# Two attention layers on one core: layer 1's value product by halves twice, its row sums on two engines, and three edits of order in every such product

## The chip, the cores and the metric

The kernel runs on one core of a Trainium2 chip. The metric is the device time of one launch in microseconds (us), as the median of three runs; less is better. A profile is one further execution.

## What is computed

Eight images of 512 channels and 1024 pixels (32 x 32) go through two attention layers, all in fp32. Layer 0 has 32 normalization groups and 8 heads, layer 1 has 8 groups and one head.

```python
# layer 0, per image
h = group_norm(x, 32 groups); q, k, v = w_qkv @ h + b
a = softmax((q * s).T @ (k * s)) @ v        # per head of 64 channels
x = x + w_proj @ a + b_proj
# layer 1
xn = group_norm(x, 8 groups)
q, k, v = (conv1x1(xn, w) for w in (q_w, k_w, v_w))
attn = softmax(einsum('bqc,bck->bqk', q, k) / sqrt(C))
x = x + conv1x1(einsum('bqk,bkc->bqc', attn, v), p_w, p_b)
```

In layer 1 the kernel multiplies the weights first: m is the product of the query and key weights, z's weight that of the value and projection weights. So it needs g = m h, the scores g h, z = h z_w, and the product of the exponentials with z, divided by the row sums.

## The kernel before

**Products in halves.** A matrix product is split in halves in each of its dimensions and made from seven products of halves instead of eight, by sums of the operands' quarters made ahead (`left_sums`, `right_sums`, lines 150 to 175) and additions to the results. Done once, this is `wino` (L222): seven steps, 1, 6, 2, 5, 7, 4, 3, on three kinds of PSUM banks a, b and c, with additions (L240, L251, L385, L387) as evictions. Done twice, it is `conv2` with `inner_steps`: four pairs of outer products, (1, 5), (2, 6), (7) and (3, 4), which its text numbers 0 to 3; each pair makes its inner steps on two outer products at a time that lie side by side in one PSUM bank.

**A pair in `inner_steps`.** Step 1 fills bank a. ScalarE copies a to b (L471), so that b goes on from the same product. Then come the previous pair's steps 3 and 4, held back in a list called `tail`, then this pair's 6, 2, 5 and 7. Step 6 adds to b and is evicted as u2, step 2 to a, step 5 fills c and is evicted as c5, step 7 adds to b and is evicted with c5. Step 3 adds to c and is evicted with u2, step 4 to b. Evictions of pair 0 are ScalarE copies (L461), the others VectorE additions (L539, with the bias L537), one for each outer product where the targets do not lie side by side, so two of 256 columns each. For pair 2 GpSimd adds results further (L544). A step 7's matmul writes bank b, so it waits until u2 has been read.

**Who uses which.** `conv2` makes layer 0's v (by tokens: image columns are the stationary operand and 128 weight columns stream), k, q and the projection p, and layer 1's g. v, k, q and p are made so 7 times, g 8 times. z is made by `by_token`, so by `wino`: 56 matmuls of 256 columns. `scores1` makes the 49 outer-inner products of the scores through `inner_steps`, with exponentials (L741) put into the hooks. `values1` is one `wino` (L828, L829 and L806 are its evictions).

**The order around z.** For image b in layer 1 and image b + 1 in layer 0 the order on TensorE is attention of layer 0, g, scores, z, the value product, then v, k, q and p. Instructions of an engine run in the order of the program where `keep_in_program_order` holds them. Small work that may lie anywhere goes to the list `background`: each step takes the first entry off it (three after a step of z). `hooks` are run after step 7 of each pair, or after a step of `wino`. z's first products lie between the last steps of the scores, and its last ones inside the value product.

**Row sums and factors.** The sums over the exponentials' rows for each of two column halves come from two quarters each (`add_up`, L745, all on GpSimd: two additions of 1024 columns, a third of 1024, one of 512). A small matmul with ones adds up over partitions. `right_sums` makes the right operand's factors from the exponentials in eight subtractions of 1024 columns (L788), four on VectorE, then four on GpSimd, which come after the sums in the `background`. The sums of z for the left operand (L157 to L160) run on VectorE.

**Weights.** Weight sums are made once at the start and kept in DRAM: `wdram` once halved (for z 1792 KB in one load), `wdram2` twice halved (1792 and 1344 KB in two loads, L337). `uses` lists the loads in their order; each `load_weight` takes the next. z's sums are made in image 0's attention, by entries of `later` indexed by the half head steps.

Of the kernel before, what the change touches and what calls it, by code (L numbers as in the profile page):

```python
# [9 lines left out]
F32 = mybir.dt.float32  # L10
# [19 lines left out]
def two_attention_blocks_kernel(  # L30
# [143 lines left out]
    def main_path(ctx):  # L174
# [124 lines left out]

        wdram2 = {n: dram.tile([P, 7, 7, P], F32, name=f"sums2_{n}") for n in "qkmvp"}  # L300

        def keep2(n, t, engine=nc.gpsimd):

            if engine is nc.gpsimd:
                u = wpool.tile([P, 4, 7, P], F32, tag="w", name=f"prepare2_{n}")
                u = [u[:, i, :, :] for i in range(4)]
            else:
                u = [big_tile(f"prepare2_{n}_{i}", (P, 7, P)) for i in range(4)]
            quarter = lambda k, i: t[:, :, k, ts(i, P)]
            a11, a21, a12, a22 = quarter(0, 0), quarter(0, 1), quarter(1, 0), quarter(1, 1)  # L310
            s1, s2, s3, s4 = u
            for dst, x, y, op in (
                (s1, a21, a22, ALU.add), (s2, s1, a11, ALU.subtract), (s3, a11, a21, ALU.subtract),
                (s4, a12, s2, ALU.subtract),
            ):
                tc.keep_in_program_order(engine.tensor_tensor(dst, x, y, op))
            for j, f in enumerate((a11, a12, s4, a22, s1, s2, s3)):
                nc.sync.dma_start(wdram2[n][:, :, j, :], f)

# [3 lines left out]
        for b in range(1, B - 1):  # L323
            uses += [*twice["m"], "z", *layer0, *twice["p"]]
        uses += ["p", *twice["m"], "z"]
        uses += [*twice["m"], "z"]
        loaded = []
# [15 lines left out]
        def weight_part(n):  # L343
            name, t = loaded.pop(0)
            assert name == n
            return t
# [93 lines left out]

        def inner_steps(uid, parity, k, mm, add, y, x, extra, after7, final, early=()):

# [22 lines left out]
            def step(j):  # L465
                if j == 1:
                    bank("a")
                    mm(ps["a"], 1, True)

                    bank("b")  # L470
                    nc.scalar.copy(ps["b"], ps["a"])  # L471
                elif j == 6:
                    mm(ps["b"], 6, False)
                    put([keep_tmp("u2", "u")], "b", (0, 1))
                    extra(0, 1, True, False)
                elif j == 2:
                    mm(ps["a"], 2, False)
                    put(y(0, 0), "a", (0, 0))
                    extra(0, 0, True, True)
                elif j == 5:  # L480
                    bank("c")
                    mm(ps["c"], 5, True)
                    put([keep_tmp("c5", "w")], "c", (1, 1))
                    extra(1, 1, True, False)
                elif j == 7:
                    mm(ps["b"], 7, False)
                    add(y(1, 1), ps["b"], [tmp["c5"]])
                    extra(1, 1, False, True)
                elif j == 3:
                    mm(ps["c"], 3, False)  # L490
                    add(y(0, 1), ps["c"], [tmp["u2"]])
                    extra(0, 1, False, True)
                elif j == 4:
                    mm(ps["b"], 4, False)
                    put(y(1, 0), "b", (1, 0))
                    extra(1, 0, True, True)
                run_background(1)
# [3 lines left out]
            for g in early:  # L501
                g()
            for j in (6, 2, 5, 7):
                step(j)
# [4 lines left out]

        def conv2(n, f, bias, name, hooks=(), after=(), by_tokens=False):  # L510

# [15 lines left out]

            def add(dst, ps, x):

                n = max(len(dst), len(x))  # L530
                for i in range(n):
                    d = dst[i] if len(dst) == n else dst[0][:, i : i + 1, :]
                    psi = ps[:, i : i + 1, :] if n > 1 else ps
                    xi = x[i] if len(x) == n else x[0][:, i : i + 1, :]
                    if isinstance(d, tuple):
                        d, oc = d
                        nc.vector.scalar_tensor_tensor(d, psi, bias[:, oc : oc + 1], xi, ALU.add, ALU.add)  # L537
                    else:
                        nc.vector.tensor_add(d, psi, xi)  # L539

# [12 lines left out]
            def pair(s, products, y, x, final):  # L553
# [20 lines left out]
                def extra(r, cc, read, done):  # L574
# [7 lines left out]
                    f"{name}_{s}", s % 2, len(products), mm, add, written, x and (lambda *at: blocks(x, *at)),  # L582
                    extra, hooks.pop(0) if hooks else (), final,
                )

            weights2 = [weight_part((n, 0))]
            pair(0, (1, 5), [(1, 0), (1, 1)], None, [])
# [124 lines left out]
        def scores1(f, gf, gsteps, first, uid, stats):  # L712
# [7 lines left out]
            total = pair_tile(f"sum_{uid}")  # L720
            parts = [pair_tile(f"sum{r}_{uid}") for r in range(2)]
            g2 = {1: first}
# [20 lines left out]
            def add_up(r, c):  # L743

                on = lambda dst, x, y: lambda: tc.keep_in_program_order(nc.gpsimd.tensor_tensor(dst, x, y, ALU.add))  # L745
                if r == c:
                    return [on(parts[r], e[c, 0, r], e[c, 1, r])]
                return [
                    *(on(parts[r], parts[r], e[c, cc, r]) for cc in range(2)),
                    on(total[:, r, :], parts[r][:, 0, :], parts[r][:, 1, :]),  # L750
                ]

            def product(s, p, y, x, before, small, after7=(), final=()):
# [24 lines left out]
            product(  # L778
                6, 4, (1, 0), (1, 0), [], stats[10:] + add_up(1, 1) + add_up(0, 1), (),
                [lambda: exps(1, 0), lambda: background.extend(add_up(1, 0) + steps)],  # L780
            )

            t = [[pair_tile(f"t{n}_{uid}_{cc}") for cc in range(2)] for n in (1, 2, 4)]
            engines = [nc.vector] * 4 + [nc.gpsimd] * 4
            fs, steps = right_sums(
                [(e[0, cc, 0], e[0, cc, 1]) for cc in range(2)], [(e[1, cc, 0], e[1, cc, 1]) for cc in range(2)],
                [lambda cc, n=n: t[n][cc] for n in range(3)],
                lambda *a: engines.pop(0).tensor_tensor(*a, ALU.subtract),  # L788
            )
            return total, {p: [x[:, i, :] for x in fs[p] for i in range(2)] for p in fs}  # L790

        def values1(b, zf, ef, r, xt, uid, hooks):
            last = b == B - 1

            def mm(p, i, ps, start):
                cut = 2 if last and (p, i) == (3, 1) else 1
                for part in range(cut):
                    cols = ts(part, HT // cut)
                    for k in range(4):
                        matmul(  # L800
                            ps[:, cols], zf[p][k // 2][:, k % 2, ts(i, P)], ef[p][k][:, cols],
                            start=start and k == 0, stop=k == 3, skip_group_check=True,
                        )
# [92 lines left out]
        def prologue():  # L896
# [46 lines left out]
            for f in p0_steps:  # L943
# [6 lines left out]
            t, steps = prepare("z")  # L950
            load = lambda: load_weight(tc.keep_in_program_order)
            later = {
                3: steps, 4: [lambda: tc.keep_in_program_order(keep("z", t)), load], 8: [load], 12: [
                    load,
                    lambda: tc.keep_in_program_order(nc.vector.tensor_copy(ubias, bias[0])),
# [85 lines left out]
        def projection2(b, inner, hooks):  # L1041

            norm = GroupNorm(1, f"1_{b}", halves=True)
            y = conv2("p", inner, obias[0], f"p_{b}", hooks)
            xt = [load_x(b, c, "x") for c in range(KC)]
# [62 lines left out]
        def layer1_rest(b, inner, gf, gsteps, stats, hooks, ahead):  # L1108
            first = query_factors(gf[1], f"1_1_{b}")
            total, ef = scores1(inner, gf, gsteps, first, f"1_{b}", stats)  # L1110
            state = {}

            def sums():
                state["r"] = reciprocals([total], f"1_{b}", True, nc.sync)

            z = by_token(
                weight("z"), hf, f"z1_{b}", hooks=[*hooks, [sums]], back=3,
                after=[load_weight, lambda: background.extend(zsteps)],
            )
            all_background()  # L1120
            xt = [load_again(b, c, "x") for c in range(KC)]
            stiles = [big_tile(f"sz{i}_{b}", (P, 2, 2, C // 2)) for i in (1, 2, 4)]
            halves = lambda t: (t[:, :, : C // 2], t[:, :, C // 2 :])
            zf, zsteps = left_sums(
                [halves(t) for t in z[:2]], [halves(t) for t in z[2:]],
                [lambda j, t=t: t[:, j, :, :] for t in stiles], nc.vector.tensor_add, nc.vector.tensor_sub,
            )
# [4 lines left out]
        for b in range(B):  # L1132
# [31 lines left out]
            if last:  # L1164
# [11 lines left out]
                ahead = [loads, *([f] for f in applies)]  # L1176
                layer1_rest(b - 1, inner, gf, gsteps, stats, [[], mean, [], affine], ahead)
                break
# [249 lines left out]
```

## Time and profile before

| what | value |
|---|---|
| median of 3 runs | 2799.11 us (2798.98 to 2799.2) |
| the profiled execution | 2799.0 us, span 2797.1 us |
| granted TensorE clock | 1.000 |
| TensorE busy | 2784.4 us, 12764 records |
| VectorE, ScalarE, GpSimd busy | 1989.0, 985.4, 1267.3 us |
| DMA | 320.10 MB, 114 GB/s |

A timeline line gives start, length, engine, line, operation, the tile written and those read, the size, and a count of records that follow each other; in brackets stands the idle time before, and who ended it. A line of a group gives the total busy time, the mean of one in ns, and the idle time before it. The chain of waits is followed back from the last instruction. The helper at L60 issues all matmuls, so they are told apart by their tiles. Each fp32 matmul leaves two records.

### The profile page before, as it was taken

What the parts mean: (1) busy time and instruction counts of PE and PEld (TensorE: products, weight loads), DVE (VectorE), ACT (ScalarE), POOL (GpSimd) and SP (SyncE); (2) the same over time, 40 slices, a digit from 0 to 9 for tenths busy, and PEclk for the clock granted to TensorE, in tenths of its full rate; (3) what the DMA queues carried; (4) which work ended last, traced back from release to release, by engine and by line L of the source; (5) the groups of instructions that cost most, each with busy time, mean ns of one, the idle gap of its engine ahead of it and who ended that gap; (6) DMA issues with size and microseconds to landing.
All of it is one profiled execution on the core that took longest, in us unless ns stands there. A gap on an engine that the chain in (4) does not pass through costs nothing.

```text
span 2797.1 us, 35099 instructions
## 1 busy us (share of the span) xinstructions
PE 2784.4 (100%) x12764; PEld 1752.8 (63%) x12764; DVE 1989.0 (71%) x3022; ACT 985.4 (35%) x1275; POOL 1267.3 (45%) x1300
## 2 busy tenths in 40 slices
PE   9999999999999999999999999999999999999999
PEld 6437637676376853858538584485844868348585
DVE  6577777667776677776786767776677766787665
ACT  1253463214531246312553125531254213633130
POOL 2303606744077430865308652185612846137672
PEclk9999999999999999999999999999999999999999
DMA  7835412344113441134401443114521035112302
GB/s 265 255 128 184 179 32 69 130 154 153 39 62 136 157 152 32 62 145 160 148 24 62 162 183 107 33 53 162 203 88 62 24 151 217 54 61 89 121 4 73
DMA packets 118669, 320.10 MB, mean 114 GB/s; under 512 B 19607, under 2 KB 58199, under 8 KB 107866
## 3 DMA queue, kind: packets, MB, share of 16 engines
q1 hardware_dynamic: 117902, 317.36, 31.9%
q8 instruction: 103, 1.69, 0.2%
q14 instruction: 76, 0.62, 0.1%
q10 hardware_dynamic: 588, 0.42, 0.0%
HBM read 247.13 MB, written 70.62 MB: 114 GB/s over the span
## 4 chain that ended last, share of the span: by engine, by line
PE 98%; DVE 1%; POOL 0%; DMA 0%; issue 0%; POOLq 0%
PE sc L60 16%; PE av L60 16%; PE psb_av L60 6%; PE psb L60 5%; PE psa_av L60 4%; PE psc_av L60 4%; PE psc L60 3%; PE psa L60 3%; PE psb_z L60 3%; PE psb_v L60 3%; PE psb_g L60 3%; PE psb_k L60 3%; PE psb_q L60 3%; PE psb_p L60 2%; PE psa_z L60 2%; PE psc_z L60 2%
## 5 line engine op out<-in xcount | busy, mean ns | idle before, releaser
L660 ACT ACTIVATE e<-sc 128x1024 f32<-128x1024 f32 x512 | 476.1, 1053 | 72.5 <-PE sc L60 72.5
L664 DVE TENSOR_TENSOR sum<-sum,e 128x1024 f32<-128x1024 f32 x384 | 470.9, 1226 | 35.2 <-ACT e L660 0.5
L60 PE MATMUL sc<-q,k 64*128 64x512 f32 x2048 | 457.0, 596 | 0.0
L60 PE MATMUL av<-e,v 128*64 128x512 f32 x2048 | 453.4, 595 | 0.0
L60 PEld LDWEIGHTS sc<-q,k 64*128 64x128 f32 x2048 | 189.9, 186 | 246.4 <-ACT e L660 121.8
L60 PEld LDWEIGHTS av<-e,v 128*64 128x64 f32 x2048 | 141.4, 137 | 299.0 <-issue 288.2
L423 POOL TENSOR_TENSOR inner_h<-x 128x256 f32<-128x256 f32 x16 | 14.8, 923 | 415.9 <-DVE x L1130 415.9
L662 DVE TENSOR_TENSOR sum<-e,e 128x1024 f32<-128x1024 f32 x64 | 79.2, 1237 | 107.5 <-ACT e L660 107.5
L683 ACT COPY a<-av 128x512 f32<-128x512 f32 x64 | 37.5, 587 | 319.3 <-PE av L60 285.4
L126 POOL TENSOR_TENSOR rstd<-ve,mhalf 128x4 f32<-128x4 f32 x16 | 16.7, 1041 | 263.2 <-DVE ve L124 263.2
L60 PE MATMUL psb<-inner,inner_h 128*128 128x256 f32 x448 | 115.6, 381 | 0.0
L60 PE MATMUL psa_av<-e,z 128*128 128x512 f32 x256 | 113.3, 596 | 0.0
L423 POOL TENSOR_TENSOR inner_h<-h 128x256 f32<-128x256 f32 x30 | 24.7, 822 | 180.4 <-DVE h L1130 112.6
L745 POOL TENSOR_TENSOR sum<-sum,e 128x1024 f32<-128x1024 f32 x32 | 81.3, 2542 | 28.7 <-ACT e L741 27.4
L60 PEld LDWEIGHTS psb<-inner,inner_h 128*128 128x128 f32 x448 | 84.5, 190 | 13.5 <-POOL inner L438 2.1
L471 ACT COPY psb_v<-psa_v 128x512 f32<-128x512 f32 (+1 forms) x28 | 14.5, 517 | 218.7 <-DVE x L806 154.9
L60 PE MATMUL psb_g<-inner_h,w_m 128*128 128x256 f32 x336 | 86.6, 385 | 0.3
L731 DVE TENSOR_TENSOR e<-psc,u 128x512 f32<-128x512 f32 x56 | 38.7, 691 | 66.2 <-PE psc L60 66.2
L544 POOL TENSOR_TENSOR v<-v,v 128x256 f32<-128x256 f32 x28 | 20.0, 726 | 144.5 <-DVE u_v L539 144.4
L60 PEld LDWEIGHTS psa_av<-e,z 128*128 128x128 f32 x256 | 48.0, 190 | 57.2 <-issue 56.6
L741 ACT ACTIVATE e<-e 128x1024 f32<-128x1024 f32 x64 | 65.1, 1052 | 46.4 <-DVE e L731 25.5
L736 POOL TENSOR_TENSOR e<-e,e 128x512 f32<-128x512 f32 x64 | 79.4, 1270 | 2.0 <-DVE e L731 1.9
(437 smaller groups left out, 6094.0 us busy)
## 6 DMA issues: line engine op xcount, KB each, us to landing
r<-all_rows SPq DMA_DIRECT2D x78, 256.0 KB
x<-in_x SPq DMA_DIRECT2D x36, 512.0 KB
h<-in_x SPq DMA_DIRECT2D x32, 512.0 KB
spill<-x SPq DMA_DIRECT2D x32, 512.0 KB
x<-spill SPq DMA_DIRECT2D x32, 512.0 KB
out<-x SPq DMA_DIRECT2D x63, 256.0 KB
kept<-a SPq DMA_DIRECT2D x28, 512.0 KB
again<-kept SPq DMA_DIRECT2D x28, 512.0 KB
```

Of the source, the lines that this page charges most:

```text
L60: tc.keep_in_program_order(nc.tensor.matmul(*args, **kw))
L126: nc.gpsimd.tensor_tensor(rstd, ve, mhalf, ALU.pow)
L423: pin(engine.tensor_tensor(dst, x, y, ALU.subtract))
L544: nc.gpsimd.tensor_tensor(d, x, y, ALU.add)
L660: nc.scalar.activation(e, sc, AF.Exp, scale=(C // 8) ** -0.5)
L662: nc.vector.tensor_add(total, es[0], e)
L664: nc.vector.tensor_add(total, total, e)
L683: nc.scalar.copy(dst, av)
L731: nc.vector.tensor_add(dst[0], ps, x[0])
L736: nc.gpsimd.tensor_tensor(blocks(dst, r, cc)[0], blocks(x, r, cc)[0], blocks(y, r, cc)[0], ALU.add)
L741: nc.scalar.activation(e[c, cc, r], e[c, cc, r], AF.Exp, scale=scale)
L745: on = lambda dst, x, y: lambda: tc.keep_in_program_order(nc.gpsimd.tensor_tensor(dst, x, y, ALU.add))
```

## The change

z is made by `conv2` by tokens. Its weight sums are halved twice: `keep2` is cut into steps which GpSimd runs at four places of image 0's attention, then seven stores. z now uses two loads of weights per image. Row sums of two quarters ((0, 0) and (1, 1)) stay on GpSimd, as three additions of 512 columns, those of the other two go to VectorE, as four each. The eight factors are all GpSimd's, two in the hook of z's pair 1 and six in that of pair 3, and stand with other signs.

In all convolutions by `conv2`: pair 1's step 4 eviction is made in two, and its second half follows the eviction of pair 2's step 6 (`defer`, `flush`); in pair 3 the copy from a to b becomes two copies, one for each outer product (`halved`). For p, pair 3's steps are 6, 5, 2, 7 (`five_first`).

```diff
-        wdram2 = {n: dram.tile([P, 7, 7, P], F32, name=f"sums2_{n}") for n in "qkmvp"}
+        wdram2 = {n: dram.tile([P, 7, 7, P], F32, name=f"sums2_{n}") for n in "qkmvpz"}
...
+        def keep2_steps(n, t, engine=nc.gpsimd, pin=lambda ins: ins):
...
+            def store():
+                for j, f in enumerate((a11, a12, s4, a22, s1, s2, s3)):
+                    pin(nc.sync.dma_start(wdram2[n][:, :, j, :], f))
...
-            uses += [*twice["m"], "z", *layer0, *twice["p"]]
+            uses += [*twice["m"], *twice["z"], *layer0, *twice["p"]]
...
                     bank("b")
-                    nc.scalar.copy(ps["b"], ps["a"])
+                    for part in [slice(i, i + 1) for i in range(k)] if halved else [slice(0, k)]:
+                        nc.scalar.copy(ps["b"][:, part, :], ps["a"][:, part, :])
                 elif j == 6:
                     mm(ps["b"], 6, False)
                     put([keep_tmp("u2", "u")], "b", (0, 1))
+                    while flush:
+                        flush.pop(0)()
...
                     mm(ps["b"], 4, False)
-                    put(y(1, 0), "b", (1, 0))
+                    if defer is None:
+                        put(y(1, 0), "b", (1, 0))
+                    else:
+                        add(y(1, 0), ps["b"], x(1, 0), (0,))
+                        defer.append(lambda: add(y(1, 0), ps["b"], x(1, 0), (1,)))
...
-            for j in (6, 2, 5, 7):
+            for j in (6, 5, 2, 7) if five_first else (6, 2, 5, 7):
...
-                    extra, hooks.pop(0) if hooks else (), final,
+                    extra, hooks.pop(0) if hooks else (), final, (), second if s == 1 else None, second if s == 2 else None, five_first=alone and s == 3, halved=s == 3,
...
-                on = lambda dst, x, y: lambda: tc.keep_in_program_order(nc.gpsimd.tensor_tensor(dst, x, y, ALU.add))
+                engine = nc.gpsimd if r == c else nc.vector
+                on = lambda *a: lambda: tc.keep_in_program_order(engine.tensor_tensor(*a, ALU.add))
+                dst, terms = total[:, r, :], [e[c, cc, r][:, i, :] for cc in range(2) for i in range(2)]
                 if r == c:
-                    return [on(parts[r], e[c, 0, r], e[c, 1, r])]
...
+                    return [on(dst, *terms[:2]), *(on(dst, dst, t) for t in terms[2:])]
+                return [on(dst, dst, t) for t in terms]
...
-                6, 4, (1, 0), (1, 0), [], stats[10:] + add_up(1, 1) + add_up(0, 1), (),
-                [lambda: exps(1, 0), lambda: background.extend(add_up(1, 0) + steps)],
+                6, 4, (1, 0), (1, 0), [], stats[10:] + add_up(1, 1), (),
+                [lambda: exps(1, 0), lambda: background.extend(add_up(0, 1) + add_up(1, 0))],
...
-            engines = [nc.vector] * 4 + [nc.gpsimd] * 4
...
+            on = lambda *a: lambda: tc.keep_in_program_order(nc.gpsimd.tensor_tensor(*a))
+            steps = [
+                on(dst[cc], x[cc], y[cc], op) for dst, x, y, op in (
+                    (b12, b22, b12, ALU.subtract), (t2, b12, b11, ALU.add), (t1, b22, t2, ALU.subtract),
+                    (t4, b21, t2, ALU.subtract),
+                ) for cc in (1, 0)
+            ]
...
-            y = conv2("p", inner, obias[0], f"p_{b}", hooks)
+            y = conv2("p", inner, obias[0], f"p_{b}", hooks, alone=True)
...
-            z = by_token(
-                weight("z"), hf, f"z1_{b}", hooks=[*hooks, [sums]], back=3,
-                after=[load_weight, lambda: background.extend(zsteps)],
+            z = conv2(
+                "z", inner, None, f"z1_{b}", [hooks[0], [*hooks[1], *esteps[:2]], [*hooks[2], sums], [*hooks[3], *esteps[2:]]],
+                after=[lambda: [f() for f in zsteps]], by_tokens=True,
             )
...
-            stiles = [big_tile(f"sz{i}_{b}", (P, 2, 2, C // 2)) for i in (1, 2, 4)]
+            stiles = [pair_tile(f"sz{i}_{b}") for i in (1, 2, 4)]
```

More of the change, by code (lines that the diff above doesn't have):

```diff
@@ L297, in keep @@
             return nc.sync.dma_start(wdram[n], t)
-        wdram2 = {n: dram.tile([P, 7, 7, P], F32, name=f"sums2_{n}") for n in "qkmvp"}
-        def keep2(n, t, engine=nc.gpsimd):
+        wdram2 = {n: dram.tile([P, 7, 7, P], F32, name=f"sums2_{n}") for n in "qkmvpz"}
+        def keep2_steps(n, t, engine=nc.gpsimd, pin=lambda ins: ins):
             if engine is nc.gpsimd:
@@ L311, in keep2 @@
             s1, s2, s3, s4 = u
[L312 to L318, printed above, removed]
+            def store():
+                for j, f in enumerate((a11, a12, s4, a22, s1, s2, s3)):
+                    pin(nc.sync.dma_start(wdram2[n][:, :, j, :], f))
+            return [
+                *(
+                    lambda dst=dst, x=x, y=y, op=op: tc.keep_in_program_order(engine.tensor_tensor(dst, x, y, op))
+                    for dst, x, y, op in (
+                        (s1, a21, a22, ALU.add), (s2, s1, a11, ALU.subtract), (s3, a11, a21, ALU.subtract),
+                        (s4, a12, s2, ALU.subtract),
+                    )
+                ),
+                store,
+            ]
+        def keep2(n, t, engine=nc.gpsimd):
+            for f in keep2_steps(n, t, engine):
+                f()
         twice = {n: [(n, 0), (n, 1)] for n in wdram2}
@@ L323, in main_path @@
         for b in range(1, B - 1):
-            uses += [*twice["m"], "z", *layer0, *twice["p"]]
-        uses += ["p", *twice["m"], "z"]
-        uses += [*twice["m"], "z"]
+            uses += [*twice["m"], *twice["z"], *layer0, *twice["p"]]
+        uses += ["p", *twice["m"], *twice["z"]]
+        uses += [*twice["m"], *twice["z"]]
         loaded = []
@@ L439, in query_factors, with inner_steps @@
             return {1: a11, 2: a12, 3: s4, 4: a22, 5: s1, 6: s2, 7: s3}
-        def inner_steps(uid, parity, k, mm, add, y, x, extra, after7, final, early=()):
+        def inner_steps(uid, parity, k, mm, add, y, x, extra, after7, final, early=(), defer=None, flush=None, five_first=False, halved=False):
             ps, tmp = {}, {}
@@ L508, in inner_steps, with conv2 @@
             tail.extend(final)
-        def conv2(n, f, bias, name, hooks=(), after=(), by_tokens=False):
+        def conv2(n, f, bias, name, hooks=(), after=(), by_tokens=False, alone=False):
             out = channel_tiles(name)
@@ L526, in blocks, with add @@
                 ]
-            def add(dst, ps, x):
+            def add(dst, ps, x, parts=None):
                 n = max(len(dst), len(x))
-                for i in range(n):
+                pin = (lambda ins: ins) if parts is None or 0 in parts else tc.keep_in_program_order
+                for i in range(n) if parts is None else parts:
                     d = dst[i] if len(dst) == n else dst[0][:, i : i + 1, :]
@@ L538, in add @@
                     else:
-                        nc.vector.tensor_add(d, psi, xi)
+                        pin(nc.vector.tensor_add(d, psi, xi))
             def more(dst, x, y, r, cc):
@@ L582, in pair @@
                     f"{name}_{s}", s % 2, len(products), mm, add, written, x and (lambda *at: blocks(x, *at)),
-                    extra, hooks.pop(0) if hooks else (), final,
+                    extra, hooks.pop(0) if hooks else (), final, (), second if s == 1 else None, second if s == 2 else None, five_first=alone and s == 3, halved=s == 3,
                 )
+            second = []
             weights2 = [weight_part((n, 0))]
@@ L720, in scores1 @@
             total = pair_tile(f"sum_{uid}")
-            parts = [pair_tile(f"sum{r}_{uid}") for r in range(2)]
             g2 = {1: first}
@@ L743, in add_up @@
             def add_up(r, c):
-                on = lambda dst, x, y: lambda: tc.keep_in_program_order(nc.gpsimd.tensor_tensor(dst, x, y, ALU.add))
+                engine = nc.gpsimd if r == c else nc.vector
+                on = lambda *a: lambda: tc.keep_in_program_order(engine.tensor_tensor(*a, ALU.add))
+                dst, terms = total[:, r, :], [e[c, cc, r][:, i, :] for cc in range(2) for i in range(2)]
                 if r == c:
-                    return [on(parts[r], e[c, 0, r], e[c, 1, r])]
[L748 to L751, printed above, removed]
+                    return [on(dst, *terms[:2]), *(on(dst, dst, t) for t in terms[2:])]
+                return [on(dst, dst, t) for t in terms]
             def product(s, p, y, x, before, small, after7=(), final=()):
@@ L778, in scores1 @@
             product(
-                6, 4, (1, 0), (1, 0), [], stats[10:] + add_up(1, 1) + add_up(0, 1), (),
-                [lambda: exps(1, 0), lambda: background.extend(add_up(1, 0) + steps)],
-            )
-            t = [[pair_tile(f"t{n}_{uid}_{cc}") for cc in range(2)] for n in (1, 2, 4)]
-            engines = [nc.vector] * 4 + [nc.gpsimd] * 4
[L785 to L790, printed above, removed]
+                6, 4, (1, 0), (1, 0), [], stats[10:] + add_up(1, 1), (),
+                [lambda: exps(1, 0), lambda: background.extend(add_up(0, 1) + add_up(1, 0))],
+            )
+            t1, t2, t4 = ([pair_tile(f"t{n}_{uid}_{cc}") for cc in range(2)] for n in (1, 2, 4))
+            b11, b12, b21, b22 = ([e[c, cc, r] for cc in range(2)] for c in range(2) for r in range(2))
+            on = lambda *a: lambda: tc.keep_in_program_order(nc.gpsimd.tensor_tensor(*a))
[4 more added lines that the diff above has]
+                ) for cc in (1, 0)
+            ]
+            fs = {1: b11, 2: b21, 3: b22, 4: t4, 5: t1, 6: t2, 7: b12}
+            return total, {p: [x[:, i, :] for x in fs[p] for i in range(2)] for p in fs}, steps
         def values1(b, zf, ef, r, xt, uid, hooks):
@@ L800, in mm @@
                         matmul(
-                            ps[:, cols], zf[p][k // 2][:, k % 2, ts(i, P)], ef[p][k][:, cols],
+                            ps[:, cols], zf[p][i][:, ts(k, P)], ef[p][k][:, cols],
                             start=start and k == 0, stop=k == 3, skip_group_check=True,
@@ L951, in prologue @@
             load = lambda: load_weight(tc.keep_in_program_order)
+            second = keep2_steps("z", t, pin=tc.keep_in_program_order)
             later = {
-                3: steps, 4: [lambda: tc.keep_in_program_order(keep("z", t)), load], 8: [load], 12: [
-                    load,
+                3: steps, 4: [load], 5: second[:1], 7: second[1:2], 9: second[2:3], 11: second[3:4], 12: [
+                    second[4], load, load,
                     lambda: tc.keep_in_program_order(nc.vector.tensor_copy(ubias, bias[0])),
@@ L1109, in layer1_rest @@
             first = query_factors(gf[1], f"1_1_{b}")
-            total, ef = scores1(inner, gf, gsteps, first, f"1_{b}", stats)
+            total, ef, esteps = scores1(inner, gf, gsteps, first, f"1_{b}", stats)
             state = {}
@@ L1121, in layer1_rest @@
             xt = [load_again(b, c, "x") for c in range(KC)]
-            stiles = [big_tile(f"sz{i}_{b}", (P, 2, 2, C // 2)) for i in (1, 2, 4)]
-            halves = lambda t: (t[:, :, : C // 2], t[:, :, C // 2 :])
+            stiles = [pair_tile(f"sz{i}_{b}") for i in (1, 2, 4)]
+            halves = lambda i, h: (z[i][:, ts(h, HT)], z[2 + i][:, ts(h, HT)])
             zf, zsteps = left_sums(
-                [halves(t) for t in z[:2]], [halves(t) for t in z[2:]],
-                [lambda j, t=t: t[:, j, :, :] for t in stiles], nc.vector.tensor_add, nc.vector.tensor_sub,
+                [halves(i, 0) for i in range(2)], [halves(i, 1) for i in range(2)],
+                [lambda j, t=t: t[:, j, :] for t in stiles], nc.vector.tensor_add, nc.vector.tensor_sub,
             )
@@ L1176, in main_path @@
                 ahead = [loads, *([f] for f in applies)]
-                layer1_rest(b - 1, inner, gf, gsteps, stats, [[], mean, [], affine], ahead)
+                layer1_rest(b - 1, inner, gf, gsteps, stats, [mean, affine, [], []], ahead)
                 break
```

## The prediction

> **What bounds the kernel now.** I read the shares by engine first, then the chain of work that ended last, then the timelines of the stages that the change touches, and last the groups of ScalarE and VectorE.
>
> ```profile
> PE 2784.4 (100%) x12764; PEld 1752.8 (63%) x12764; DVE 1989.0 (71%) x3022; ACT 985.4 (35%) x1275; POOL 1267.3 (45%) x1300
> ...
> PE 98%; DVE 1%; POOL 0%; DMA 0%; issue 0%; POOLq 0%
> ```
>
> TensorE is never idle for long and carries 98% of the chain. So only two things count: fewer or shorter matmuls, and the small stalls of TensorE where it waits for an eviction. In the records a matmul of 256 columns costs 0.216 us, one of 128 columns 0.112 us (two records for each fp32 matmul).
>
> The timeline of TensorE where image 2's value product z lies (its x8 and x16 count records):
>
> ```profile
> 844.50 3.62 PE L60 MATMUL psa_z<-w_z,x 128*128 128x256 f32 x16
> ...
> 849.68 3.62 PE L60 MATMUL psb_z<-w_z,t_h 128*128 128x256 f32 x16
> 853.14 3.62 PE L60 MATMUL psa_z<-w_z,x 128*128 128x256 f32 x16
> 856.59 3.62 PE L60 MATMUL psc_z<-w_z,t_h 128*128 128x256 f32 x16
> ```
>
> Each block starts 3.46 us after the last, 16 x 0.216: z has no stall. All its blocks are 3.46 + 13.91 + 6.91 = 24.28 us.
>
> The same view in v, which is already made by `conv2` by tokens:
>
> ```profile
> 933.08 0.61 PE L60 MATMUL psc_v<-w_v,inner_h 128*128 128x128 f32 x4
> 933.69 0.68 PE L60 MATMUL psb_v<-w_v,inner_h 128*128 128x128 f32 x4
> 934.21 0.61 PE L60 MATMUL psa_v<-w_v,h 128*128 128x128 f32 x4
> ```
>
> Four records take 0.45 us, but 0.61 and 0.52 lie between these starts: 0.24 us lost before and at pair 2's step 7. I call this stall A. In the records it is 0.285 in g, 0.236 v, 0.22 k, 0.221 q, 0.284 p. A smaller one, B, sits in the x12 block that begins pair 3 (the matmul waits for the copy psa to psb): 0.126 g, 0.092 v, 0.063 k, 0.064 q, 0.126 p.
>
> The end of p (TensorE alone):
>
> ```profile
> 1002.88 1.03 PE L60 MATMUL psc_p<-inner_a,w_p 128*128 128x256 f32 x4
> 1003.75 1.03 PE L60 MATMUL psb_p<-inner_a,w_p 128*128 128x256 f32 x4
> 1004.83 0.70 PE L60 MATMUL psc_p<-again,w_p 128*128 128x256 f32 x2
> 1005.36 0.59 PE L60 MATMUL psc_p<-t_a,w_p 128*128 128x256 f32 x2
> 1005.79 1.08 PE L60 MATMUL psb_p<-inner_a,w_p 128*128 128x256 f32 x4
> ```
>
> Step 3 starts 1.08 after step 7 where 0.86 is work, and its first records are stretched: 0.32 us, stall C. VectorE shows why:
>
> ```profile
> 1002.32 0.76 DVE L539 TENSOR_TENSOR u_p<-psb_p,p 128x256 f32<-128x256 f32 x2 [0.67 <-PE psb_p L60]
> 1003.15 0.88 DVE L537 SCALAR_TENSOR_TENSOR p<-psa_p,obias,p 128x256 f32<-128x256 f32 x2
> 1004.02 0.76 DVE L539 TENSOR_TENSOR c_p<-psc_p,p 128x256 f32<-128x256 f32 x2
> 1004.81 0.88 DVE L537 SCALAR_TENSOR_TENSOR p<-psb_p,obias,c_p 128x256 f32<-128x256 f32 x2
> ```
>
> Four evictions u, a, c, b run back to back; step 3 waits for c (ends 1004.78), step 4 for b (ends 1005.69; step 4 starts 1005.79).
>
> [...] Each copy of pair 3 fills halves of one bank, and in the changed kernel's instruction order the first matmul of step 6 indeed waits for the second half copy. The trace of before shows no halved copy. [...]
>
> ```profile
> L664 DVE TENSOR_TENSOR sum<-sum,e 128x1024 f32<-128x1024 f32 x384 | 470.9, 1226 | 35.2 <-ACT e L660 0.5
> ...
> L788 DVE TENSOR_TENSOR t<-e,t 128x1024 f32<-128x1024 f32 x16 | 45.7, 2893 | 0.0
> L731 DVE TENSOR_TENSOR e<-psc,u 128x512 f32<-128x512 f32 x56 | 38.7, 691 | 66.2 <-PE psc L60 66.2
> ```
>
> An SBUF addition of 1024 takes 1.23 where GpSimd is mostly idle and 2.89 in z, while it works. The PSUM ones are 0.69 all over.
>
> **Part 1: z in halves twice (8 times).** Removed: 24.28 us of TensorE. Added: 98 matmuls of 128 columns, 196 records. v, the same function, takes 0.89 + 19.53 + 1.78 = 22.20 us; less its A and B, 21.87. To that I add three stalls.
> - Pair 3's copy: B with v's size and the halving (below), 0.09 + 0.18 = 0.27.
> - Z1. ScalarE now has two exponentials in front of the copy u2 of pair 0. Score steps 3 and 4 come right after z's shorter step 1 (845.39 to 847.11), the additions end 847.21, the exponentials run 847.25 to 849.25 (2.00 for two, as now), the copy ends 849.80, TensorE follows 0.14 later at 849.94. Step 7 could start at 849.80. With about 0.07 for the restart (as in A): 0.2.
> - Z2. The row sums come to VectorE: 8 additions of 512 instead of none, while 4 additions of 1024 (L788, 10.2 us) go to GpSimd. They are built in among z's evictions: three before pair 0's step 7 eviction, then two, one, two, and one after pair 1's u2. At 0.67 each, 0.70 when dependent, and 0.69 and 0.76 for evictions, pair 1's c5 ends 858.26, so TensorE goes on at 858.4; pair 1's step 3 is due at 857.65. That is 0.83 at these sizes, 0.4 if each sum takes 0.62; I take 0.75.
>
> Sum 21.87 + 0.27 + 0.2 + 0.75 = 23.09 instead of 24.28: 1.19 each, **-9.5 us** in 8 (bounds -5 and -13; without any stall it would be -19).
>
> What is hidden here: GpSimd makes all eight factors of the right side, 8 x 2.35 = 18.8 us, the last near 881, needed from 884.9 on, and two pair 2 and 3 additions of z lie between (3.4 us early). The scaling behind them ends near 884 instead of 873, and the inner factors of h at about 911 where v takes them at 920. Were that cover gone, each us late costs a us. z's own left sums on VectorE are ready near 882.4, needed from 883.6. Weights: one load of 1792 KB becomes two, 3136 KB, queued where v's are today; SyncE is not late. Image 0 has seven more stores and four GpSimd steps in the attention stage: 13.7 us of SyncE issue at 1.96 us each, after which v's second weights land about 240, needed 247. Once only; uncovered, some 5 us.
>
> **Part 2: moved addition.** Pair 1's second half addition goes behind pair 2's u2, which step 7 waits for. u2 then ends 0.3 earlier (0.34 us pitch of a half), in p at 998.35 against a due time of 998.58 less 0.14: stall A goes. Next late would be c5, which isn't due. 8 x 0.285 + 7 x (0.236 + 0.22 + 0.221 + 0.284) = **-9.0 us**. If only the wait shrinks, -6.
>
> **Part 3: halved copy.** The groups of ScalarE give both sizes:
>
> ```profile
> L471 ACT COPY psb_p<-psa_p 128x512 f32<-128x512 f32 x21 | 12.0, 570 | 20.7 <-PE psa_p L60 20.7
> ...
> L471 ACT COPY psb_p<-psa_p 128x256 f32<-128x256 f32 x7 | 2.5, 357 | 23.5 <-PE psa_p L60 23.5
> ```
>
> The first half still waits for all of step 1, the second for the first, and TensorE for the second. So 0.570 becomes 2 x 0.357 and a gap of some 0.03: +0.18. [...] For the 36 convolutions there are: **+6.5 us** (3.6 to 9). Those of z are counted in part 1.
>
> **Part 4: exchanged products in p (7 times).** Steps 6, 5, 2, 7: c moves ahead of a, so step 3 needn't wait. But u, c, a, b is still 0.83 + 0.83 + 0.83 + 0.88 back to back, b still ends near 1005.72, and step 4 waits for it at 1005.8 as now. The stall moves from step 3 to step 4: **+0.4 us**, between -1.5 and +1.
>
> Sum -9.5 - 9.0 + 6.5 + 0.4 = -11.6. The profiled execution took 2799.0 us (span 2797.1 and 1.9 around it), 0.1 from the median 2799.11: **2787.5 us**. Own range, all bounds that may fall together: 2781 to 2795.
>
> **Rivals.**
> - All edits work as meant (6%). For it: evictions are all that the stalls wait for. Against: the wait for the second half. Then z gains 24.28 - 21.87 - 0.95 = 1.46 each (11.7), B vanishes (8 x 0.126 + 7 x 0.345 = 3.4), C too (2.2): -26.3, 2772.8 us.
> - z gains nothing (20%). For it: VectorE and ScalarE take on work just where z's evictions got shorter in between, and one more stall of 1.2 us in any of the later pairs eats it. Against: the order shows none. -9.0 + 6.5 + 0.4 = -2.1: 2797.0 us.
> - Slower (12%): VectorE's eight row sums, each of two SBUF operands, run into GpSimd's own sums and factors between 848 and 857 and take half of the 2.3 of L788, 1.17 instead of 0.67. For it: L788 itself, in this place. Against: the factors start only after the last sum, and GpSimd's sums of (1,1) are nearly through. 8 x 0.5 = 4.0 more in front of c5, all on the path: z loses 2.8 each, 22.5 in all: 2819.5 us. It decides from 0.94 us per sum on (z 0.96 worse).
>
> **Numbers.** Forecast 62%, rivals 6, 20 and 12%. A difference of 0.2% (5.6 us) is about what a measurement of this kernel can tell from no change: faster is below 2793.5, slower above 2804.7. The forecast and the first rival are faster: 0.68; z without gain is the same: 0.20; slower 0.12. The range goes from the forecast's 2781 to 2798.5, past the second rival, and leaves out 18%.
>
> **What would show it.** z's records at 0.112 with a gap at pair 0's step 7 of 0.2 and before pair 1's step 3 near 0.8; sums near 0.7; pair 2's step 7 in all convolutions without a gap; two 0.357 copies and a gap before pair 3's step 6 grown by 0.18; in p the gap at step 4. Wrong would be sums over 0.94, gaps in av for late left sums, or a wait at g for weights.

## The result, and the profile after

The changed kernel takes 2814.22 us (median of 5, 2811.59 to 2814.88) beside 2799.11 us: a ratio of 1.0052, 95% interval 1.0041 to 1.0063. It is 15.1 us slower; 2787.5 were predicted, with a range up to 2798.5. Its profiled span is 2812.4 us, 15.3 longer than before.

The shares by engine and the chain of waits on the page of the changed kernel:

```profile
PE 2780.0 (99%) x13436; PEld 1763.5 (63%) x13436; DVE 2037.4 (72%) x3214; ACT 1006.4 (36%) x1351; POOL 1295.1 (46%) x1384
...
PE 93%; DVE 5%; issue 1%; DMA 1%; SPq 0%; POOL 0%; DVEq 0%; POOLq 0%
```

TensorE has less to do than before (2780.0 us instead of 2784.4), but VectorE now holds 5% of the chain instead of 1%. To find the place, I summed the distances from each TensorE record's start to the next by the tiles that they write (us in the whole span, before and after). Here z is what the title calls the value product, and "value product" from here on is the later product of the exponentials with z, whose tiles are psa_av, psb_av and psc_av:

| stage | before | after | change |
|---|---|---|---|
| z | 194.30 | 180.43 | -13.87 |
| g, v, k, q, p together | 882.32 | 879.36 | -2.96 |
| scores, attention | 1241.65 | 1241.41 | -0.24 |
| value product | 385.49 | 417.66 | +32.17 |

The sum, +15.1, is the loss but for 0.2 of the span's 15.3. It lies in a stage whose own products and evictions the change leaves as they were; only z's layout in its left operand, and the place where the program issues the left sums of z, differ. The timeline of all engines there, for image 2 (the last two columns tell the count, and the idle time ahead of an instruction with who ended it):

```profile
872.16 9.28 POOL L803 TENSOR_TENSOR t<-e,t 128x1024 f32<-128x1024 f32 x4
...
881.40 2.36 POOL L718 TENSOR_TENSOR a<-a,r 128x1024 f32<-128x1024 f32 x1
...
882.01 3.44 DVE L157 TENSOR_TENSOR sz<-z 128x512 f32<-128x512 f32 x2
...
883.73 1.17 POOL L434 TENSOR_TENSOR inner_h<-h 128x256 f32<-128x256 f32 x1
...
884.46 7.10 PE L60 MATMUL psc_av<-t,sz 128*128 128x512 f32 x16 [0.46 <-DVE sz L157]
...
897.73 2.34 DVE L171 TENSOR_TENSOR t_h<-h,t_h 128x512 f32<-128x512 f32 x2
898.35 1.17 POOL L434 TENSOR_TENSOR inner_h<-h,h 128x256 f32<-128x256 f32 x1
899.48 1.17 POOL L434 TENSOR_TENSOR inner_h<-h,inner_h 128x256 f32<-128x256 f32 x1
899.99 0.68 DVE L240 TENSOR_TENSOR u_av<-psb_av,t_av 128x512 f32<-128x512 f32 x1
...
900.72 8.82 PE L60 MATMUL psb_av<-e,z 128*128 128x512 f32 x16 [2.29 <-DVE u_av L240]
```

The same stretch before (L423 and L698 are now L434 and L718):

```profile
870.90 2.35 POOL L698 TENSOR_TENSOR a<-a,r 128x1024 f32<-128x1024 f32 x1
882.38 1.22 POOL L423 TENSOR_TENSOR inner_h<-h 128x256 f32<-128x256 f32 x1 [9.13 <-ACT h L138]
...
890.36 4.65 POOL L423 TENSOR_TENSOR inner_h<-t_h 128x256 f32<-128x256 f32 x1 [3.22 <-DVE t_h L168]
...
893.15 1.28 DVE L171 TENSOR_TENSOR t_h<-h,t_h 128x512 f32<-128x512 f32 x2
...
895.40 0.69 DVE L240 TENSOR_TENSOR u_av<-psb_av,t_av 128x512 f32<-128x512 f32 x1 [0.97 <-PE psb_av L60]
...
898.64 7.03 PE L60 MATMUL psb_av<-e,z 128*128 128x512 f32 x16
```

VectorE makes z's eight left sums (L157 to L160) and then eight image factors of the next h (L168 to L171). The two of L171 take 2.34 us now and took 1.28 before. Beside them GpSimd works with one pause, of 3.70 us; its own subtractions of 256 columns last 1.17 instead of 0.73. So u for step 7, behind them in VectorE's queue, is done only at 900.67, and TensorE, which left step 6 at 898.43, idles for 2.29 us. Before, u waited for TensorE and TensorE did not wait.

Then 16 records take 8.82 us that take 7.03 elsewhere. The view of stretches shows the granted clock (PEclk, ahead of the last two columns):

```profile
core 0: us, PE busy (x) PEld busy (x) DVE busy (x) ACT busy (x) POOL busy (x), PEclk, DMA share, GB/s
896.00:900.70 4.70, 2.43 (x6) 0.76 (x4) 4.70 (x6) 0.00 (x0) 4.70 (x6) 1.00 0.87 321
900.70:904.30 3.60, 3.58 (x5) 1.59 (x6) 3.60 (x8) 0.00 (x0) 3.60 (x6) 0.53 0.00 0
```

Behind the idle stretch the clock is half for some 3.4 us, and a record of 512 columns takes 0.853 us instead of 0.430. Over seven images the loss, beyond the usual 0.430 from record to record, is: 0.62 before step 5 in six of them (3.7), 2.44 before step 7 in six and 3.25 in the last (17.9), slow records in six (1.8 each, 10.8). That is 32.4 where the sum has 32.2; the first records of a few blocks, up to 0.1 us longer at other places than before, are the difference.

### The profile page after: what moved, and what is told of

Read it like the earlier page. It is cut to its first block, busy times and chain, and to the rows that moved or that the text cites. A ratio compares the mean times of both kernels' runs of the same rounds, so it can differ in the third digit from the quotient of the medians.

```text
span 2812.4 us, 36985 instructions
## 1 busy us (share of the span) xinstructions
PE 2780.0 (99%) x13436; PEld 1763.5 (63%) x13436; DVE 2037.4 (72%) x3214; ACT 1006.4 (36%) x1351; POOL 1295.1 (46%) x1384
## 4 chain that ended last, share of the span: by engine, by line
PE 93%; DVE 5%; issue 1%; DMA 1%; SPq 0%; POOL 0%; DVEq 0%; POOLq 0%
PE sc L60 16%; PE av L60 16%; PE psb L60 5%; PE psb_av L60 5%; PE psc L60 3%; PE psa L60 3%; PE psb_v L60 3%; PE psa_av L60 3%; PE psb_g L60 3%; PE psb_q L60 3%; PE psb_k L60 3%; PE psb_z L60 3%; PE psb_p L60 2%; PE psc_av L60 2%; PE psc_v L60 2%; PE psa_v L60 2%
## 5 line engine op out<-in xcount | busy, mean ns | idle before, releaser
L434 POOL TENSOR_TENSOR inner_h<-x 128x256 f32<-128x256 f32 x16 | 14.7, 920 | 415.9 <-DVE x L1153 415.9
L483 ACT COPY psb_v<-psa_v 128x256 f32<-128x256 f32 (+1 forms) x35 | 15.5, 442 | 256.1 <-DVE x L828 193.6
L60 PE MATMUL psb_z<-w_z,inner_h 128*128 128x128 f32 x672 | 89.1, 277 | 0.0
L60 PE MATMUL psb_av<-e,z 128*128 128x512 f32 x128 | 67.1, 685 | 16.8 <-DVE u_av L240 16.8
L60 PEld LDWEIGHTS psb_z<-w_z,inner_h 128*128 128x128 f32 x672 | 82.0, 192 | 1.6
```

The costliest lines, as they stand in the source:

```text
L60: tc.keep_in_program_order(nc.tensor.matmul(*args, **kw))
L434: pin(engine.tensor_tensor(dst, x, y, ALU.subtract))
L483: nc.scalar.copy(ps["b"][:, part, :], ps["a"][:, part, :])
```

## Experiments

Each runs against the kernel before on the same chip. Theory A: the loss is VectorE's additions of two SBUF operands, stretched because GpSimd now works at the same time (L171's two take 2.34 us instead of 1.28); the idle time of 2.29 us and the half clock of 3.4 us follow from it. The rival B is named in each expectation.

**Part 1 alone.** Edit: `halved=False`, `five_first=False`, and `None, None` for the two lists of the moved addition.

> Part 1 alone (z in halves twice, shared row sums), without the moved addition, the halved copy and the exchanged products. Theory A (the whole loss comes from part 1, through the value product's evictions): z gains about 14 us, the value product loses about 32, so 2799 + 18 = 2817 us, some 3 us over the changed kernel. Rival B (the order edits of parts 2 to 4 cost the time): below 2799 us.

Measured: 2817.38 us (1.0066, 1.0050 to 1.0083). The value product takes 417.77 us, z 180.37. The loss belongs to part 1; the three edits of order together gain 3.2.

**Left sums first.** VectorE's order is forced: the sums ahead of the first eviction of step 2 (L851).

```diff
-                [lambda j, t=t: t[:, j, :] for t in stiles], nc.vector.tensor_add, nc.vector.tensor_sub,
+                [lambda j, t=t: t[:, j, :] for t in stiles],
+                lambda *a: tc.keep_in_program_order(nc.vector.tensor_add(*a)),
+                lambda *a: tc.keep_in_program_order(nc.vector.tensor_sub(*a)),
...
-                nc.vector.tensor_mul(o, o, r[:, c, :])
+                mul = nc.vector.tensor_mul(o, o, r[:, c, :])
+                if (row, c) == (0, 0) and not last:
+                    tc.keep_in_program_order(mul)
```

> The changed kernel with VectorE's eight left sums of z pinned ahead of the value product's first evictions (step 2), so that they start near 878 instead of 882 in image 2. Theory A (order in VectorE's queue, plus additions stretched to 1.2 us while GpSimd works): the sums end 3 to 4 us earlier, u for step 7 comes in time, the wait of 2.4 us and the slow records behind it go in all seven images: -25 to -32 us, 2782 to 2789 us. Rival B (the wait comes from GpSimd's later work alone, the order does not matter): the sums are stretched as much and end at the same time, under 5 us gained, about 2810 us.

Measured: 2820.71 us (1.0076, 1.0059 to 1.0093), slower than both said. VectorE's timeline of that kernel:

```profile
881.82 4.54 DVE L1152 TENSOR_TENSOR sz<-z 128x512 f32<-128x512 f32 x2
886.29 3.97 DVE L1153 TENSOR_TENSOR sz<-sz,z 128x512 f32<-128x512 f32 x2
890.18 2.34 DVE L1153 TENSOR_TENSOR z<-z,z 128x512 f32<-128x512 f32 x2
```

The second of these sums and the GpSimd instruction beside it, from all engines of that kernel:

```profile
883.00 2.82 POOL L803 TENSOR_TENSOR t<-e,t 128x1024 f32<-128x1024 f32 x1
...
883.51 2.85 DVE L1152 TENSOR_TENSOR sz<-z 128x512 f32<-128x512 f32 x1
```

Earlier sums meet GpSimd's last factor of 1024 columns (until 885.82) and its scaling, and one of them then takes 2.85 us, beside subtractions of 256 columns 1.21. So an earlier place in the queue is no remedy while GpSimd's long instructions lie there, and my expectation of A was wrong in taking 1.2 us for all company: a sum lasted as long as the GpSimd instruction beside it. The wait before step 5 is gone, but the one before step 7 grew from 2.9 to 4.0 us from record to record.

**GpSimd held back.** A one-column copy on GpSimd reads VectorE's last image factor; the inner factors of h stand behind it. First in six images, then also with the scaling of the last heads (`scaled`) and in the seventh.

```diff
-                made["inner"], inner = inner_factors(hf, uid)
+                made["inner"], inner = inner_factors(hf, uid, tc.keep_in_program_order)
+                mark = small.tile([P, 1], F32, tag="mark", name=f"mark_{uid}")
+                gate = lambda: tc.keep_in_program_order(nc.gpsimd.tensor_copy(mark, hf[4][1][:, 0:1]))
                 hooks[1] += applies[:1]
-                hooks[2] += [applies[1], inner[0], *t[:2]]
-                hooks[3] += [*applies[2:], inner[1], *t[2:4]]
-                hooks[4] += [*inner[2:4], lambda: background.extend([*t[4:6], *inner[4:6], *t[6:], inner[6]])]
+                hooks[2] += [applies[1], *t[:2]]
+                hooks[3] += [*applies[2:], *t[2:4]]
+                hooks[4] += [*t[4:], gate, *inner[:4], lambda: background.extend(inner[4:])]
```

> The changed kernel with GpSimd's inner factors of h held back until VectorE's last image factor is made (a one-column copy ahead of them that reads it). The order on VectorE stays. Theory A (VectorE's additions of two SBUF operands are stretched from 0.67 to 1.2 us by GpSimd): the sums and image factors fall to 0.67 from 884 on, u is in time for step 7, so the wait and the slow records go: -25 to -30 us, 2784 to 2789 us; the wait of 0.6 before step 5 stays, since GpSimd's scaling still lies there. Rival B (they are late because of their place in the queue alone): durations stay, no gain.

Measured: 2790.74 us (0.9970, 0.9959 to 0.9982). The idle time before step 7 and the slow records are gone in six images; 0.65 before step 5 and the seventh image's 5 us stay.

> The changed kernel with GpSimd held back in all seven images: its inner factors of h and its scaling of the last heads stand behind VectorE's image factors (a one-column copy ahead of them), for the last image too. Theory A (GpSimd's company is what makes VectorE late): what was left with six images gated goes too, the 0.65 us before step 5 in six images (the scaling lay there) and the 4.8 us of the seventh: 2790.7 - 3.9 - 4.8 = 2782 us. Rival B (something else holds step 5): 2786 us or more, the 0.65 stays.

Measured: 2781.15 us (0.9936, 0.9923 to 0.9950), 33 us under the changed kernel. The value product takes 384.70. VectorE's timeline of it in image 2:

```profile
878.26 1.28 DVE L157 TENSOR_TENSOR sz<-z 128x512 f32<-128x512 f32 x2
...
887.94 1.28 DVE L171 TENSOR_TENSOR t_h<-h,t_h 128x512 f32<-128x512 f32 x2
890.59 0.69 DVE L240 TENSOR_TENSOR u_av<-psb_av,t_av 128x512 f32<-128x512 f32 x1 [1.36 <-PE psb_av L60]
```

The same instructions in the same order take 1.28 a pair, and u now waits for TensorE instead of the other way round. GpSimd does the work that was held back later, and TensorE does not wait for it. That is A. DMA traffic is no rival: in the kernel before it moved 223 GB/s from 888 to 894.5 us beside image factors of 1.28 a pair, and 207 from 882 to 890 in the changed kernel beside the slow sums.

**Control: the kernel before, held back in the same way.**

> A control: the kernel before with the same holding back of GpSimd as in the gated kernels. Theory A (the kernel before has no wait in the value product that GpSimd causes): within 2 us of 2799. Rival B (the holding back is a gain by itself, whatever the change did): 2785 us or less.

Measured: 2799.13 us (1.0002, 0.9993 to 1.0010). Holding GpSimd back is no gain by itself; it repairs what the change did.

**Which piece of part 1.** The changed kernel with row sums and factors as they were (L745 and L788 of before), z still in halves twice.

> The changed kernel with the row sums and the factors of the right side as they were (sums on GpSimd, four factors on VectorE and four on GpSimd, L788), so z in halves twice without the shared row sums. Theory A (the value product's loss comes from GpSimd's eight factors and what they push back): GpSimd is free near 874 again, the value product loses nothing (-30 us against the changed kernel). But four subtractions of 2.3 to 2.9 us now stand among z's evictions on VectorE: pair 1's u2 ends near 863 where step 7 needs it at 856, some 7 us for each of 8 images: 2814 - 30 + 56 = 2840 us. Rival B (z in halves twice is itself what makes the value product late): the waits before its steps 5 and 7 stay.

Measured: 2851.26 us (1.0189, 1.0173 to 1.0204). The value product is free of loss (384.70), and z takes 250.00 us instead of 180.43. TensorE in z there:

```profile
860.31 1.06 PE L60 MATMUL psc_z<-w_z,inner_h 128*128 128x128 f32 x8
867.43 2.08 PE L60 MATMUL psb_z<-w_z,inner_h 128*128 128x128 f32 x8 [6.06 <-DVE u_z L558]
```

So the change of row sums and factors is needed for z: with the four long subtractions on VectorE z takes 8.7 us more an image. The clock again falls behind the idle time (8 records in 2.08 us instead of 1.06, and a mean clock of 0.989 in the profiled execution), which my 7 us an image had left out.

The other half needs care, because VectorE's order differs too: here the left sums come ahead of step 2's evictions and start 0.95 us after the step's first matmul, in the changed kernel 5.04 us after it. The kernel with the left sums forced to the front is the one to compare with: they start as early there (0.94), but meet GpSimd's long instructions, and the eight take 12.4 us instead of 7.0. The inner factors of h stretch the image factors in this run as well (L171 takes 2.34 a pair), and u is still in time. So neither part of GpSimd's later work brings the wait before step 7 by itself: not the inner factors with the early order (this run), and not the factors and the scaling with the changed kernel's order (the kernel with six images held back, where only 0.65 before step 5 stayed).

**Is the clock lowered by idleness?** Matmuls that nobody reads fill the wait before step 7, 2.15 us or 0.86.

```diff
+                if (p, i) == (7, 0) and not last:
+                    unused = acc_tile(f"unused_{uid}")
+                    for n in range(3):
+                        cols = slice(0, HT) if n < 2 else slice(0, HT // 2)
+                        matmul(
+                            unused[:, cols], zf[6][0][:, ts(0, P)], ef[6][0][:, cols], start=True, stop=True,
+                            skip_group_check=True,
+                        )
```

> The changed kernel with five extra halves' worth of matmuls (2.15 us, into a bank that nobody reads) ahead of step 7 of the value product in seven images: they fill the wait for u. Theory A (the records of 0.85 us instead of 0.43 behind the wait are a lower granted clock, and it falls because TensorE stood idle): step 7 starts as before, but its records take 0.43: 7 x 1.8 = -12.6 us, 2801.6 us, clock 1.000. Rival B (the slow records come from contention with other engines' traffic at this place): no gain, 2814 us or more.

Measured: 2805.98 us (1.0026, 1.0017 to 1.0036), clock 1.000. More work made the kernel 8.2 us faster. The slow records are gone, so they were a lower clock and not contention; in the trace of the changed kernel they are 10.8 us in six images, so the 12.6 expected for seven was too much.

> The changed kernel with one matmul of 512 columns (0.86 us) ahead of step 7 of the value product in seven images: it fills a part of the wait and leaves TensorE idle for about 1.5 us instead of 2.3. Theory A (the granted clock falls after an idle stretch of about 2 us or more): no slow records, as with the 2.15 us of matmuls: about 2804 us. Rival B (any idle stretch of over 1 us brings the half clock): 7 x 1.8 us of slow records stay, 2814 us.

Measured: 2805.72 us (1.0023, 1.0014 to 1.0031): 1.42 us idle in six images bring no slow record.

**Halved copy.** Edit: `halved=False` in the kernel with GpSimd held back.

> The kernel with GpSimd held back in all images, with pair 3's copy as one of 128x512 again instead of two halves. Theory A (TensorE waits for the second half, so halving only lengthens): each of 44 convolutions gets back what the trace shows as the growth of stall B, 0.13 to 0.18 us: -5.7 to -8 us against the halved one in the same call. Rival B (the halves help or are neutral): no change, or slower by up to 3 us.

Measured: 2775.45 us (0.9916, 0.9902 to 0.9930), 5.7 less than with the halves. ScalarE in p of the changed kernel, and TensorE there:

```profile
1003.77 0.75 ACT L483 COPY psb_p<-psa_p 128x256 f32<-128x256 f32 x2 [1.34 <-PE psa_p L60]
...
1004.00 1.72 PE L60 MATMUL psb_p<-inner_a,w_p 128*128 128x256 f32 x6
```

The two halves last 0.75 where one copy lasts 0.57, and the block of six records takes 1.72 instead of 1.58. Halving only costs.

**Exchanged products.** Edit: `five_first=False`.

> The kernel with GpSimd held back in all images, with p's pair 3 in the old order 6, 2, 5, 7. Theory A (the exchange moves the stall from step 3 to step 4, since VectorE's four evictions run back to back either way): within 1.5 us of the exchanged one in the same call, and if anything faster, since the trace shows 0.53 us at step 4 where there were 0.37 in both. Rival B (the exchange saves its 0.32 us in 7 images): 2.2 us slower.

Measured: 2781.33 us (0.9937, 0.9924 to 0.9951), beside 2781.15 with the exchange. No difference. TensorE at the end of p in the changed kernel:

```profile
1007.28 1.03 PE L60 MATMUL psb_p<-inner_a,w_p 128*128 128x256 f32 x4
1008.14 0.59 PE L60 MATMUL psc_p<-again,w_p 128*128 128x256 f32 x2
1008.58 0.59 PE L60 MATMUL psc_p<-t_a,w_p 128*128 128x256 f32 x2
1009.43 1.13 PE L60 MATMUL psb_p<-inner_a,w_p 128*128 128x256 f32 x4 [0.26 <-DVE p L556]
```

Step 3 follows step 7 at once, and step 4 waits instead, for the eviction of step 7.

**Moved addition.** Edit: `None, None` in place of the two lists.

> The kernel with GpSimd held back in all images, with pair 1's second addition back in its old place, ahead of pair 2's u2, in all 44 convolutions. Theory A (moving it removes stall A, 0.22 to 0.285 us each): slower by 9.0 us and some 2 more for z, 10 to 11 us, against the moved one in the same call. Rival B (the stall would have been hidden by the next one): less than 4 us.

Measured: 2790.73 us (0.9970, 0.9959 to 0.9982), 9.6 more than with it.

**What pays, together.** GpSimd held back, one copy, the old order in p.

> GpSimd held back in all images, pair 3's copy in one piece, and p's pair 3 in the old order: the parts of the change that the runs so far show to pay. By the single results: 2781.15 - 5.7 + 0.2 = 2775.6 us, 0.8% below the kernel before and 1.4% below the changed one. Over 2778 us would mean that the single edits do not add up.

Measured: 2774.82 us (0.9914, 0.9901 to 0.9928), 0.9% below the kernel before and 39 us below the changed one. The single results add up.

## Why the prediction was wrong

**z itself.** Forecast -9.5, measured -13.87, past the bound of -13. The form of the sum was right, the stalls were too large: Z1 0.09 instead of 0.2, Z2 0.14 instead of 0.75, pair 3's copy 0.21 instead of 0.27 (image 2's records); around the matmul of the row sums 0.2 were lost that the sum had not. Z2 is the term that was mis-sized. Its sizes, added end to end, give 7.07 us from pair 0's step 7 eviction to the end of c5 (three evictions of about 0.76, two of 0.69, five sums); the trace has 6.41 (851.84 to 858.25), since each VectorE instruction starts up to 0.08 before the recorded end of the one before it. The list of places in the prediction also counts nine sums; there are eight, three, two, two and one. The slower rival was that GpSimd would stretch these sums; they took 0.71 or less, because GpSimd waited for them: its factors start at 857.07. That the rival's 2819.5 lies near the measured time is luck; its cause did not occur.

**Moved addition.** -9.0 for 36 convolutions and some 2 for z; measured 9.6 for all. Stall A is gone in the trace of the changed kernel. Right.

**Halved copy.** +6.5 and 1.4 within z; measured 5.7 for all. Right in sign and in what TensorE waits for. In the changed kernel's p above the two halves ran one behind the other, 0.75 us together; the second ended at 1004.52, and step 6's first matmul started at 1004.62.

**Exchanged products.** +0.4, measured within 0.2 of nothing. Right: the stall moved to step 4.

**What is hidden here.** This step failed. It says that GpSimd's eight factors, the scaling behind them "near 884 instead of 873" and the left sums of z "ready near 882.4, needed from 883.6" are hidden. The times of GpSimd were right: the scaling ended at 883.76, and the inner factors reached v in time. The left sums were late: VectorE began them at 882.01, behind step 2's first eviction, and the first took 2.31 us beside the scaling and ended at 884.32, where step 5 was due at 883.84 (6.87 after step 2's start). I asked only whether GpSimd's results come in time, and costed its busy time at nothing for its neighbour. Before, GpSimd was idle from 873 to 882 and began five subtractions of 256 columns between there and 894, and VectorE made 14 of its 16 sums and image factors in 0.68 us each and two in 1.2. After, GpSimd was busy from 872 on but for 3.7 us, and eleven of the 16 took 1.21 us or more. These 16 stand in one queue with u, which step 7 needs, so VectorE's delay ran into the path: +32.2 us, the lower clock behind the idle time included, where the sum had 0. The prediction had a sign of this in its trace, L788's 2.89 us beside the 1.23 of an addition where GpSimd was mostly idle, and had used it for one place, the row sums in z, where the order of data forbids the overlap. It was not used for the place to which the change moves GpSimd's work. With the term of 32 us, and z and the other convolutions as measured, the sum comes to 2799.1 - 13.9 - 3.0 + 32.2 = 2814.4.

The order on VectorE (step 2's eviction ahead of the left sums, VectorE idle for 2.61 us before it) costs nothing with GpSimd out of the way: the kernel with GpSimd held back has that order, and no block of its value product starts late. What stays open: no run cuts GpSimd's factors of 1024 columns into shorter ones, so that this would be a second remedy is not shown.

## What to carry to other kernels

When work moves to another engine, look at the whole stretch in which that engine is then busy, and price every neighbour's instruction there that the traces show slower beside it, not only whether the moved results come in time. For VectorE and GpSimd that means: list VectorE's instructions with two SBUF operands in that stretch (1.21 to 2.85 us here instead of 0.68), and see who stands behind them in its queue. GpSimd's work had slack here, and a one-column copy that waits for VectorE's last instruction was enough to take them apart (33 us for seven small copies).

## What the runs showed of the hardware

- A VectorE addition of 512 columns from SBUF took 0.68 us alone, 1.21 beside GpSimd subtractions of 256 columns and 2.85 beside one of 1024. GpSimd's took 1.17 instead of 0.73 and 2.82 instead of 2.35. From 893 to 900 us in the changed kernel the two engines' instructions start one for one, each engine's 1.13 us after its last; GpSimd's long instructions were the dear ones for VectorE. It isn't always VectorE that loses: in the kernel before, a subtraction of GpSimd that began at 890.36 took 4.65 us while VectorE went on at 0.68. Additions with a PSUM operand stayed at 0.69 (858.34 us in the changed kernel, beside L803 on GpSimd).
- In the changed kernel the granted clock was half for 3.41 us, at 1.8 us a time, behind six of the seven waits of 2.27 to 3.09 us without a matmul; behind 1.42 us in the run with the short filler it was not. The length of the wait alone does not decide it: one image of the changed kernel had the same wait (2.28 us) and no slow record, nor had the seventh with the short filler (2.28 us idle). In the changed kernel the half stretches begin at 900.73, 1245.48, 1590.23, 1934.97, 2279.72 and 2648.36 us, each 344.75 us after the last, and at the end 368.64: 101 and 108 times 3.413 us, the length of each of them. They do not keep time with the work: step 7 begins 344.46 to 344.62 us after the last one in the four images with the spacing of 344.75, so the half stretches begin 0.01 to 0.94 us behind its first matmul. In the 3.41 us ahead of each of these starts TensorE was idle for 2.27 us or more. Counted back from 900.73 by 101 times 3.413 us, a start would lie at 555.99, by my estimate: inside the wait of the image without slow records (555.64 to 557.92), of which 1.93 us come after it. In the lines, whose columns are those of the view of stretches above, the first is the 3.41 us that hold the wait and the others are two half stretches:

```profile
897.31:900.73 3.42, 1.14 (x4) 0.20 (x2) 3.42 (x5) 0.00 (x0) 3.42 (x4) 1.00 0.83 314
900.73:904.14 3.41, 3.41 (x4) 1.50 (x5) 3.41 (x7) 0.00 (x0) 3.41 (x6) 0.50 0.00 0
1245.48:1248.89 3.41, 3.41 (x5) 1.33 (x6) 3.41 (x8) 0.00 (x0) 3.41 (x6) 0.50 0.00 0
```
